# Four graph layers on one core: order and buffers at the seams, joined 64x64 sections, and attention weights divided before they are used

## The chip, the cores and the metric

The kernel runs on one core of one Trainium2 chip. Its time is the device time of one execution in microseconds (us); with one core this is the time of the slowest core. The engines are TensorE (PE; its weight loads are listed as PEld), VectorE (DVE), ScalarE (ACT), GpSimd (POOL) and SyncE (SP, which issues most DMAs). All data is fp32.

## The reference, cut to what matters

There are 128 graphs of 64 nodes with 512 features, 8192 tokens in all. Each of four layers takes `h = relu(layernorm(x))` and adds its result to x:

```python
# layer 0: one weight per node, softmax over the nodes of a graph
w = inv_scale * mask * sum_d(q * (adj @ (k * mask)));  x += softmax(w) * v
# layer 1: weight[i, j] = adj * exp(q_i . k_j), divided by its row sum
x += (weight / weight.sum(axis=2, keepdims=True)) @ value
# layer 2: eight heads of 64, scores times (adj + adj), softmax, output weights Wo
# layer 3: alpha = A * exp(leaky_relu(sj + si + ab)); transition = alpha / (sum + 1e-12)
H = X @ Wk[0] + (tr @ X) @ Wk[1] + (tr @ tr @ X) @ Wk[2] + bk;  x += relu(H)
```

## The kernel before, in words

The tokens form 32 blocks (`n_blk`) of 256: two tiles (`TT`) of 128 tokens, and each tile holds two graphs (`g`). Layers 0 and 1 alternate by pairs of blocks (list `steps`: layer 0 of blocks 0 and 1, layer 1 of blocks 0 and 1, layer 0 of blocks 2 and 3, and so on). Then layer 2 runs over all blocks, and layer 3 over all blocks. x goes to HBM between layers 1, 2 and 3.

Each 512x512 product is a `Product`: seven products of half size on combinations (`sums` of the block on POOL, `formed` or `chore` for the weights). `first`, `second` and `late` issue them, one `add` being four PE records of 128x256 or eight of 128x128; `keep_ab` and `keep_dc` read the PSUM banks in between, and `store`, `store_T` and `add_to` at the end. `side_by_side` runs two products together and calls the lists in `between`: the first list amid `first` and `second` of the first product, the others before each `late`.

Small matrices per graph are multiplied in the 64x64 form: `neighbour_sums` gives `pa` in layer 0, `po` in layer 1 (named po1 in the code) and `po` in layer 3 (po2 and po3 in the code). Layer 1's scores `sc` (`products`) have the form 128x64, layer 2's scores and contexts 64x64. `graph_sums` multiplies by a block diagonal of ones (form 128x128). Layer 1 makes `e` (the weights), sums its rows with four 64x1 products `den`, and scales the output by the reciprocal; layer 3 does so with `al`, in `layer3_tail` for po2, and the same reciprocal `r` serves `layer3_end` for po3.

PSUM has eight banks: pools `ps_tr` (2, transposes and small results), `ps_mm` (4, products) and `ps_sc` (2, scores and sums). Buffers in SBUF are named by tags and counts; a new tile waits for the oldest holder of its tag. The instruction order of each engine comes from a planner that follows the program's order as a priority and its own model of times; `tc.issue_after(ins)` puts what is traced inside it behind `ins` on that engine.

Names in the prediction's steps: `setup1` (L446) loads layer 1's q and k weights, makes nine dot products with the biases (L467), transposes both weights (`transpose_weight`, L416 to L422) and multiplies them (`folded`, L430). `add_to` (L333) is layer 2's residual addition. `setup3` (L733) multiplies `L3_WvT` by the two attention columns (`pu`). `layer3_norm` (L777) loads, normalises and makes the dots `hu` (L788), `di` and `sj`; `layer3_in` makes `sm_i` from di, then al, then in a second stage the transposes. `layer3_step` runs head, tail and the end of the block before.

## Time and profile before

| | |
|---|---|
| median of three runs | 2678.71 us (2675.41 to 2680.66) |
| the profiled execution | 2679.86 us, span 2678.1 us |
| mean granted clock of TensorE | 0.996 |
| PE busy, share of the span | 2639.5 us, 99% |
| DVE / ACT / POOL busy | 1702.8 / 947.7 / 1288.7 us |
| a pair of blocks in layers 0 and 1, from `den` to `den` | 60.22 us |
| a step of layer 3, from `den` to `den`, median | 21.98 us |

A row of the timeline has the start, the duration, the engine, the line, the operation, what it writes and reads, its form (`64*64` is the part of the array used), shapes and the number of merged records; an idle time and its releaser stand in brackets. Durations of matmuls overlap, so what a group costs is read from the distance to the next start. In the list of waits the three numbers are the total, the count and the longest.

### The profile page before, as it was taken

What the parts mean: (1) busy time and instruction counts of PE and PEld (TensorE: products, weight loads), DVE (VectorE), ACT (ScalarE), POOL (GpSimd) and SP (SyncE); (2) the same over time, 40 slices, a digit from 0 to 9 for tenths busy, and PEclk for the clock granted to TensorE, in tenths of its full rate; (3) what the DMA queues carried; (4) which work ended last, traced back from release to release, by engine and by line L of the source; (5) the groups of instructions that cost most, each with busy time, mean ns of one, the idle gap of its engine ahead of it and who ended that gap; (6) DMA issues with size and microseconds to landing.
All of it is one profiled execution on the core that took longest, in us unless ns stands there. A gap on an engine that the chain in (4) does not pass through costs nothing.

```text
span 2678.1 us, 52780 instructions
## 1 busy us (share of the span) xinstructions
PE 2639.5 (99%) x20752; PEld 2253.1 (84%) x20752; DVE 1702.8 (64%) x4398; ACT 947.7 (35%) x2290; POOL 1288.7 (48%) x1585
## 2 busy tenths in 40 slices
PE   8999999999999999999999999999899999999999
PEld 5888888888888889999999999999777777777776
DVE  5566666666666676566566566566566666666664
ACT  2333334333333333333333333333323333333332
POOL 3443333333433335656655655655464444445544
PEclk9999999999999999999999999999999999999999
DMA  5200111111111122111111111111111111111110
GB/s 158 67 35 34 35 35 35 42 43 35 50 34 35 34 66 78 45 45 39 45 45 39 45 45 39 45 45 45 65 50 51 51 51 51 51 51 51 51 50 32
DMA packets 103165, 129.80 MB, mean 48 GB/s; under 512 B 40835, under 2 KB 50051, under 8 KB 102917
## 3 DMA queue, kind: packets, MB, share of 16 engines
q1 hardware_dynamic: 102340, 125.38, 13.9%
q8 instruction: 163, 2.67, 0.4%
q10 hardware_dynamic: 576, 1.05, 0.1%
q14 instruction: 86, 0.70, 0.1%
HBM read 76.07 MB, written 50.34 MB: 47 GB/s over the span
## 4 chain that ended last, share of the span: by engine, by line
PE 81%; POOL 6%; DVE 5%; DMA 4%; ACT 3%; issue 2%; ACTq 0%; POOLq 0%; SPq 0%; DVEq 0%
PE ab_v L251 11%; PE ab_y L251 9%; PE dc_v L251 8%; PE dc_y L251 6%; PE ab_g L244 4%; PE ab_k L244 4%; PE ab_g L251 4%; PE ab_q L244 4%; PE tr L190 3%; PE dc_g L244 3%; PE dc_g L251 3%; PE po L392 3%; PE dc_k L244 3%; PE ab_o L251 3%; PE dc_q L244 3%; DMA x<-x 2%
## 5 line engine op out<-in xcount | busy, mean ns | idle before, releaser
L179 ACT ACTIVATE h<-x,nmr,rstd 128x512 f32<-128x512 f32 x256 | 194.4, 806 | 219.6 <-DVE nmr L174 211.0
L172 POOL TENSOR_TENSOR rstd<-ve,neghalf 128x2 f32<-128x2 f32 x128 | 89.8, 701 | 365.6 <-DVE ve L170 365.4
L167 DVE BATCH_NORM_STATS2 stats<-x 128x6 f32<-128x512 f32 x256 | 165.3, 677 | 74.6 <-DMA x<-x 68.4
L251 PE MATMUL ab_y<-L_Wk,hT 128*128 128x256 f32 x768 | 207.5, 393 | 4.1 <-DVE u_y L303 2.6
L251 PEld LDWEIGHTS ab_y<-L_Wk,hT 128*128 128x128 f32 x768 | 136.4, 190 | 77.4 <-issue 25.2
L251 PE MATMUL ab_v<-L_Wv,hT 128*128 128x256 f32 x768 | 200.7, 384 | 0.0
L251 PE MATMUL ab_y<-L_Wk,S 128*128 128x256 f32 x768 | 197.8, 380 | 0.0
L251 PE MATMUL dc_v<-L_Wv,S 128*128 128x256 f32 x768 | 197.3, 379 | 0.0
L251 PE MATMUL ab_v<-L_Wv,S 128*128 128x256 f32 x768 | 197.1, 379 | 0.0
L251 PE MATMUL dc_y<-L_Wk,S 128*128 128x256 f32 x768 | 192.9, 380 | 1.3 <-DVE u_y L859 1.2
L251 PEld LDWEIGHTS dc_y<-L_Wk,S 128*128 128x128 f32 x768 | 145.2, 190 | 23.2 <-DVE u_y L859 3.7
L251 PEld LDWEIGHTS ab_v<-L_Wv,S 128*128 128x128 f32 x768 | 145.9, 190 | 19.8
L880 POOL TENSOR_TENSOR tz<-tz,y 128x512 f32<-128x512 f32 x63 | 91.5, 1452 | 146.0 <-ACT tz L877 146.0
L251 PEld LDWEIGHTS ab_y<-L_Wk,S 128*128 128x128 f32 x768 | 144.1, 191 | 18.5
L251 PEld LDWEIGHTS dc_v<-L_Wv,S 128*128 128x128 f32 x768 | 143.4, 190 | 18.9 <-issue 0.8
L251 PEld LDWEIGHTS ab_v<-L_Wv,hT 128*128 128x128 f32 x768 | 135.9, 190 | 15.4
L190 PE MATMUL tr<-ident,h 128*128 128x128 f32 x1024 | 134.4, 275 | 0.0
L190 PEld LDWEIGHTS tr<-ident,h 128*128 128x128 f32 x1024 | 119.5, 142 | 10.5
L216 POOL TENSOR_TENSOR S<-hT 128x256 f32<-128x256 f32 x128 | 101.1, 790 | 35.0 <-ACT hT L193 34.7
L219 POOL TENSOR_TENSOR S<-hT 128x256 f32<-128x256 f32 x128 | 107.9, 843 | 1.2
L306 POOL TENSOR_TENSOR gv<-u_g,p_g 128x256 f32<-128x256 f32 x32 | 23.4, 730 | 174.4 <-DVE u_g L303 174.4
L217 POOL TENSOR_TENSOR S<-S,hT 128x256 f32<-128x256 f32 x128 | 101.0, 789 | 11.6 <-DVE ve L170 10.3
(238 smaller groups left out, 6433.8 us busy)
## 6 DMA issues: line engine op xcount, KB each, us to landing
x<-x SPq DMA_DIRECT2D x128, 512.0 KB, 3.5
x<-in_x_dram SPq DMA_DIRECT2D x32, 512.0 KB, 3.6
out_dram<-x SPq DMA_DIRECT2D x31, 512.0 KB, 2.8
adjT<-in_adjT_dram SPq DMA_DIRECT2D x64, 64.0 KB, 1.9
adjq<-in_adj_dram SPq DMA_DIRECT2D x64, 64.0 KB, 2.3
L_Wk<-in_L_Wk_dram SPq DMA_DIRECT2D x16, 256.0 KB, 4.7
L_Wv<-in_L_Wv_dram SPq DMA_DIRECT2D x12, 256.0 KB, 5.3
q<-in_L_Wqk_dram ACTq DMA_DIRECT2D x4, 256.0 KB, 6.1
```

The costliest lines, as they stand in the source:

```text
L167: nc.vector.bn_stats(stats[:, t, :], x[:, t, :])
L172: nc.gpsimd.tensor_tensor(rstd, ve, neghalf, ALU.pow)
L179: nc.scalar.activation(h, x[:, t, :], AF.Relu, bias=nmr[:, t : t + 1], scale=rstd[:, t : t + 1])
L190: nc.tensor.transpose(pt[:, k, :], h[:, k * P : (k + 1) * P], ident)
L216: nc.gpsimd.tensor_tensor(S1, A21, A22, ALU.add)
L217: nc.gpsimd.tensor_tensor(S2, S1, A11, ALU.subtract)
L219: behind[0] = nc.gpsimd.tensor_tensor(S3, A11, A21, ALU.subtract)
L244: nc.tensor.matmul(dst[:, m * P : (m + 1) * P], w[:, place, k, m * P : (m + 1) * P], left[:, k, :], start=key not in self.begun, stop=last ...
L251: nc.tensor.matmul(dst, left[:, k, :], w[:, place, k, :], start=key not in self.begun, stop=last and k == 1, skip_group_check=True,)
L306: nc.gpsimd.tensor_tensor(y[:, 1, F:], self.u3, self.p5, ALU.add)
L392: nc.tensor.matmul(ps[t][half[g ^ t]], e[half[g], t, :], us[t][half[g]], start=True, stop=True)
L880: nc.gpsimd.tensor_tensor(tz[t], tz[t], y0[:, t, :], ALU.add)
```

## The change

The transposes of layer 1's q and k weights get different PSUM banks, and ACT copies all of q's; the nine dot products are made during block 0's products, and layer 0's end of block 0 is issued amid the folding. In layers 1 and 3 the weights `e` and `al` are divided by their sums ahead of use: `graph_sums`, a reciprocal of 128x128 and a product replace `den` and the scaling at the output. Layer 1's neighbour sums are issued ahead of the next odd block's `sc` or `pa` (`before`), layer 3's po3 ahead of the next block's po2. Layer 2's additions on DVE come ahead of POOL's second addition to the same part. `L3_WvT` is loaded into other buffers, `sm_i` and the division get later places, and layer 3's dots are split from its norm and issued behind the block's last read of PSUM. The first block's `am` and `msc` are issued behind the first norm's steps.

```diff
+    behind_norm = {}
     def norm(x, name: str):
...
-        nc.gpsimd.tensor_tensor(rstd, ve, neghalf, ALU.pow)
+        by_rows = nc.gpsimd.tensor_tensor(rstd, ve, neghalf, ALU.pow)
...
-        nc.vector.scalar_tensor_tensor(nmr, mv[:, :, 0], -1.0, rstd, ALU.mult, ALU.mult)
+        scaled = nc.vector.scalar_tensor_tensor(
+            nmr, mv[:, :, 0], -1.0, rstd, ALU.mult, ALU.mult
+        )
+        behind_norm.setdefault(0, (by_rows, scaled))
...
-            nc.gpsimd.tensor_tensor(x[:, 1, :F], self.u3, x[:, 1, :F], ALU.add)
-            nc.vector.tensor_tensor(x[:, 0, F:], self.c, x[:, 0, F:], ALU.add)
...
+            self.taken = nc.vector.tensor_tensor(x[:, 0, F:], self.c, x[:, 0, F:], ALU.add)
+            nc.gpsimd.tensor_tensor(x[:, 1, F:], self.u3, x[:, 1, F:], ALU.add)
...
-                x[:, 1, F:], self.u3, x[:, 1, F:], ALU.add
+                x[:, 1, :F], self.u3, x[:, 1, :F], ALU.add
...
     def side_by_side(*parts, between=()):
...
-    def transpose_weight(w, name: str):
-        pts = [ps_mm.tile([P, K, P], FP, tag="mm", name=f"tw_{name}_{m}") for m in range(K)]
+    def transpose_weight(w, name: str, places=((ps_mm, "mm"),) * K, on_scalar=(1, 3)):
+        pts = [
+            pool.tile([P, K, P], FP, tag=tag, name=f"tw_{name}_{m}")
+            for m, (pool, tag) in enumerate(places)
+        ]
...
-            if m % 2:
+            if m in on_scalar:
...
-    def folded(aT, bT, layer: int, place: int):
+    elsewhere = ((ps_tr, "tr"), (ps_sc, "sc")) * 2
+    def folded(aT, bT, layer: int, place: int, amid=lambda: None):
...
+            if not i:
+                amid()
...
     def setup0():
...
-        nc.vector.tensor_scalar(msc, mcol, -(float(D) ** -0.5), None, ALU.mult)
+        with tc.issue_after(behind_norm[0][1].ins):
+            nc.vector.tensor_scalar(msc, mcol, -(float(D) ** -0.5), None, ALU.mult)
...
     def setup1():
...
+        dots((d, bias[:, 0], 1))
+        dots(*((u[:, k : k + 1], x, 1) for k, x in enumerate(columns(qT))))
+        yield
+        dots(*((cc[:, k : k + 1], x, 0) for k, x in enumerate(columns(kT))))
...
-        for w, c in zip((qT, kT), "qk"):
-            transpose_weight(w, f"{c}1")
-        m = folded(kT, qT, 1, 2)
+        yield
+        transpose_weight(qT, "q1", on_scalar=range(K))
+        transpose_weight(kT, "k1", elsewhere)
+        m = folded(kT, qT, 1, 2, lambda: layer0_end(0, *softmax))
...
         yield m, u, c1, d, w1v, w2
-    def layer0(b: int, x, adjT, hs, hT, between):
+    def layer0(b: int, x, adjT, hs, hT, between, before):
...
-        am = small.tile([P, TT, N], FP, tag="am", name=f"am_{b}", bufs=2)
-        nc.gpsimd.tensor_tensor(
-            am,
-            adjT,
-            mcol[:, b * TT : (b + 1) * TT].unsqueeze(2).to_broadcast([P, TT, N]),
-            ALU.mult,
-        )
-        pa = [ps_tr.tile([P, D], FP, tag="tr", name=f"pa_{b}_{t}") for t in range(TT)]
+        am = small.tile([P, TT, N], FP, tag="am", name=f"am_{b}", bufs=3)
+        with tc.issue_after(behind_norm[0][0].ins):
+            nc.gpsimd.tensor_tensor(
+                am,
+                adjT,
+                mcol[:, b * TT : (b + 1) * TT].unsqueeze(2).to_broadcast([P, TT, N]),
+                ALU.mult,
+            )
+        before()
+        pa = [
+            pool.tile([P, D], FP, tag=tag, name=f"pa_{b}_{t}")
+            for t, (pool, tag) in enumerate((
+                ((ps_sc, "sc"), (ps_sc if b % 2 else ps_mm, "sc" if b % 2 else "mm"))
+                if b else ((ps_tr, "tr"),) * 2
+            ))
+        ]
...
-    def layer1(b: int, x, adjT, hs, hT, between):
+    def layer1(b: int, x, adjT, hs, hT, between, before):
...
+        before()
...
+    def layer1_divided(b: int, e):
+        den = graph_sums(e.rearrange("p t i -> p (t i)"), TT * N, f"1_{b}")
+        r = small.tile([P, TT, N], FP, tag="r", name=f"r1_{b}", bufs=2)
+        nc.vector.reciprocal(r.rearrange("p t i -> p (t i)"), den)
+        nc.vector.tensor_tensor(e, e, r, ALU.mult)
     def layer1_end(b: int, x, v, e, to):
-        po = [ps_sc.tile([P, D], FP, tag="sc", name=f"po1_{b}_{t}") for t in range(TT)]
-        den = [ps_tr.tile([P, 1], FP, tag="tr", name=f"den1_{b}_{t}") for t in range(TT)]
-        for t in range(TT):
-            for g in range(2):
-                nc.tensor.matmul(
-                    den[t][half[g ^ t]], e[half[g], t, :], ones_bd[half[g], g * N : g * N + 1],
-                    start=True, stop=True,
-                )
-        parts = neighbour_sums(po, e, [v[:, t, :] for t in range(TT)])
-        r = small.tile([P, TT], FP, tag="r1", name=f"r1_{b}")
-        for t in range(TT):
-            nc.vector.reciprocal(r[:, t : t + 1], den[t])
-        for t, out_at, at in parts:
-            nc.vector.scalar_tensor_tensor(
-                x[out_at, t, :], po[t][at], r[at, t : t + 1], x[out_at, t, :], ALU.mult, ALU.add
-            )
+        po = [ps_tr.tile([P, D], FP, tag="tr", name=f"po1_{b}_{t}") for t in range(TT)]
+        for t, out_at, at in neighbour_sums(po, e, [v[:, t, :] for t in range(TT)]):
+            nc.vector.tensor_tensor(x[out_at, t, :], po[t][at], x[out_at, t, :], ALU.add)
...
-        cT = big.tile([P, K, T], FP, tag="hT", name=f"cT_{b}")
+        cT = big.tile([P, K, T], FP, tag="hT" if b + 1 < n_blk else "v", name=f"cT_{b}")
...
-        halves = []
-        for i in range(2):
-            w = big.tile([P, K // 2, D], FP, tag="v", name=f"w3vT_{i}")
-            nc.sync.dma_start(
-                w,
-                a["L3_WvT"][i * D // 2 : (i + 1) * D // 2, :].rearrange("(k p) o -> p k o", p=P),
-            )
-            halves.append(w)
+        pair = big.tile([P, 2, D], FP, tag="v", name="w3vT")
+        chunks = [pair[:, k, :] for k in range(2)] + [
+            med.tile([P, D], FP, tag="agg", name=f"w3vT_{k}", bufs=2) for k in range(2, K)
+        ]
+        for k, w in enumerate(chunks):
+            nc.sync.dma_start(w, a["L3_WvT"][k * P : (k + 1) * P, :])
...
-            for to, x in ((pu, halves[k // 2][:, k % 2, :]), (pc, bv[:, k : k + 1])):
+            for to, x in ((pu, chunks[k]), (pc, bv[:, k : k + 1])):
...
-        us2 = big.tile([2, D + 1], FP, tag="v", name="us2")
-        nc.scalar.copy(us2[:, :D], pu)
-        nc.scalar.copy(us2[:, D:], pc)
+        us2 = med.tile([2, D], FP, tag="h", name="us2", bufs=6)
+        cs2 = small.tile([2, 1], FP, tag="cc", name="cs2", bufs=1)
+        nc.scalar.copy(us2, pu)
+        nc.scalar.copy(cs2, pc)
...
-        nc.sync.dma_start(urow, us2)
+        nc.sync.dma_start(urow[:, :D], us2)
+        nc.sync.dma_start(urow[:, D:], cs2)
...
     def layer3_norm(b: int, source):
...
+        return x, adjT, norm(x, f"3_{b}")
+    def layer3_dots(b: int, x, adjT, hs):
...
-        hs = norm(x, f"3_{b}")
...
-        al = small.tile([P, TT, N], FP, tag="am", name=f"al_{b}", bufs=2)
+        al = small.tile([P, TT, N], FP, tag="am", name=f"al_{b}", bufs=3)
...
         yield
         made.append((x, al, sums(transposed(hs, f"3_{b}"), f"3_{b}")))
+        yield
+        den = graph_sums(al.rearrange("p t i -> p (t i)"), TT * N, f"al_{b}")
+        r = small.tile([P, TT * N], FP, tag="r", name=f"r3_{b}", bufs=2)
+        nc.vector.tensor_scalar(r, den, 1e-12, None, ALU.add)
+        nc.vector.reciprocal(r, r)
+        nc.vector.tensor_tensor(al, al, r.rearrange("p (t i) -> p t i", t=TT), ALU.mult)
         yield
     def layer3_head(b: int, ops, between):
...
         p.first(ops, w3[0])
+        yield
         p.second(ops, w3[0])
-        den = [ps_tr.tile([P, 1], FP, tag="tr", name=f"den3_{b}_{t}") for t in range(TT)]
-        for t in range(TT):
-            for g in range(2):
-                nc.tensor.matmul(
-                    den[t][half[g ^ t]], al[half[g], t, :], ones_bd[half[g], g * N : g * N + 1],
-                    start=True, stop=True,
-                )
+        yield
         po = [ps_sc.tile([P, D], FP, tag="sc", name=f"po2_{b}_{t}") for t in range(TT)]
         parts = neighbour_sums(po, al, [y[:, 1, t, :] for t in range(TT)])
-        r = small.tile([P, TT], FP, tag="r1", name=f"r3_{b}")
-        for t in range(TT):
-            nc.vector.tensor_scalar(r[:, t : t + 1], den[t], 1e-12, None, ALU.add)
-        nc.vector.reciprocal(r, r)
         for t, to, at in parts:
-            nc.vector.scalar_tensor_tensor(
-                y[to, 0, t, :], po[t][at], r[at, t : t + 1], y[to, 0, t, :], ALU.mult, ALU.add
-            )
+            nc.vector.tensor_tensor(y[to, 0, t, :], po[t][at], y[to, 0, t, :], ALU.add)
...
-        nc.vector.tensor_tensor(y0[:, 0, F:], p.c, p.u2, ALU.add)
+        kept = nc.vector.tensor_tensor(y0[:, 0, F:], p.c, p.u2, ALU.add)
...
-        yield r, y0
-    def layer3_end(b: int, x, al, y, r, y0):
-        po = [ps_sc.tile([P, D], FP, tag="sc", name=f"po3_{b}_{t}") for t in range(TT)]
+        yield y0, kept
+    def layer3_end(b: int, x, al, y, y0):
+        po = [ps_tr.tile([P, D], FP, tag="tr", name=f"po3_{b}_{t}") for t in range(TT)]
...
         for t, out_at, at in neighbour_sums(po, al, [y[:, 0, t, :] for t in range(TT)]):
             if last and not t:
-                nc.vector.scalar_tensor_tensor(
-                    tz[t], po[t], r[:, t : t + 1], y0[:, t, :], ALU.mult, ALU.add
-                )
+                nc.vector.tensor_tensor(tz[t], po[t], y0[:, t, :], ALU.add)
...
-                nc.scalar.activation(tz[t][out_at], po[t][at], AF.Copy, scale=r[at, t : t + 1])
+                nc.scalar.copy(tz[t][out_at], po[t][at])
...
-    transpose_weight(f0[1], "k0")
+    transpose_weight(f0[1], "k0", ((ps_sc, "sc"),) * 2 + ((ps_mm, "mm"),) * 2)
...
-    open_end = []
...
     for i, (layer, b) in enumerate(steps):
...
+        between = [[], [chore], []]
+        if i == 0:
+            for n in (1, 2):
+                between[n].append(lambda: next(setup))
...
+            begun = []
             made1 = next(setup)
-        between = [[], [chore], []]
-        for n, end in open_end:
+        for n, end in begun:
...
+        begun = []
         if i + 1 < len(steps):
...
         if layer == 0:
-            softmax = layer0(b, *loaded[b], *normed[i], between)
-            open_end = [(0, lambda b=b, softmax=softmax: layer0_end(b, *softmax))]
+            softmax = layer0(b, *loaded[b], *normed[i], between, open_end if b % 2 else nothing)
+            begun = [(0, lambda b=b, softmax=softmax: layer0_end(b, *softmax))]
         else:
-            attention = layer1(b, *loaded[b], *normed[i], between)
-            open_end = [
-                (1, lambda b=b, a=attention: layer1_end(b, loaded[b][0], *a, x1[b]))
-            ]
-            if b == n_blk - 2:
-                open_end.append((1, lambda: fetch2(2)))
+            v, e = layer1(b, *loaded[b], *normed[i], between, open_end if b % 2 else nothing)
+            begun = [(1, lambda b=b, e=e: layer1_divided(b, e))]
+            def open_end(b=b, v=v, e=e):
+                layer1_end(b, loaded[b][0], v, e, x1[b])
+                if b == n_blk - 2:
+                    fetch2(2)
...
     def layer3_step(b: int, ahead: bool = True):
+        nonlocal normed3
...
         stages = layer3_in(b + 1, *normed3, made_in) if b + 1 < n_blk else iter(())
...
-            next(stages, None)
             if b + 2 < n_blk and ahead:
                 normed3 = layer3_norm(b + 2, x2[b + 2])
-        y = layer3_head(b, ops, [[begin], [ending.pop()], [lambda: next(stages, None)]])
+        y = layer3_head(b, ops, [
+            [begin], [], [lambda: next(stages, None), lambda: next(stages, None)]
+        ])
         yield
         tail = layer3_tail(b, al, ops, y)
         next(tail)
         yield
-        r_y0 = next(tail)
-        ending.append(lambda: layer3_end(b, x, al, y, *r_y0))
+        next(stages, None)
+        next(tail)
+        yield
+        ending.pop()()
+        next(tail)
+        yield
+        y0, kept = next(tail)
+        ending.append(lambda: layer3_end(b, x, al, y, y0))
+        if b + 2 < n_blk and ahead:
+            with tc.issue_after(kept.ins):
+                normed3 = layer3_dots(b + 2, *normed3)
         yield
...
-        [lambda: prepare2(1), chore], [*(end for _, end in open_end), chore], [lambda: turned2(1)]
+        [lambda: prepare2(1), chore], [begun[0][1], chore], [open_end, lambda: turned2(1)]
...
             stages = layer3_in(0, *normed3, made_in)
-            next(stages)
         if b + 1 < n_blk:
-            qk, ops = layer2_in(b + 1, normed2[b + 1], [[], [lambda: chore(1 if b else 2)]])
+            qk, ops = layer2_in(b + 1, normed2[b + 1], [
+                [], [lambda: chore(1 if b else 2), lambda: next(stages, None)]
+            ])
...
         else:
-            next(parts)
+            for _ in range(3):
+                next(parts)
         (of_o,) = side_by_side(part)
...
+        next(stages, None)
         nc.sync.dma_start(tokens(x2[b]), x)
...
-        if b >= n_blk - 3:
-            normed3 = layer3_norm(b - n_blk + 3, x2[b - n_blk + 3])
+        if n_blk - 3 <= b < n_blk - 1:
+            normed3 = layer3_dots(
+                b - n_blk + 3, *layer3_norm(b - n_blk + 3, x2[b - n_blk + 3])
+            )
+        elif b == n_blk - 1:
+            with tc.issue_after(of_o.taken.ins):
+                normed3 = layer3_dots(2, *layer3_norm(2, x2[2]))
```

`dots` issues the same `scalar_tensor_tensor` with `accum_out` as before, and `nothing` does nothing.

## The prediction

> **What bounds the kernel now.** I read the page first, then the waits of PE, then PE's timeline through the places that they name, and last the windows for the granted clock.
>
> ```profile
> PE 2639.5 (99%) x20752; PEld 2253.1 (84%) x20752; DVE 1702.8 (64%) x4398; ACT 947.7 (35%) x2290; POOL 1288.7 (48%) x1585
> ```
>
> TensorE sets the time; nothing else passes two thirds. A gain has to come off PE's own row: idle time, work at half clock, or time that one of its instructions takes only because of its neighbours. Waits of PE:
>
> ```profile
> PE sm_i L400 <- DVE di L793: 3.4, 1, 3.4
> PE tw_k L416 <- DVE q L422: 3.3, 1, 3.3
> PE ab_y L251 <- DVE u_y L303: 2.6, 1, 2.6
> PE pu L754 <- DMA w3vT<-in_L_WvT_dram: 2.6, 1, 2.6
> PE tr L690 <- ACT hT L193: 1.7, 1, 1.7
> PE ab_k L244 <- DVE x L341: 1.7, 8, 0.2
> PE dc_y L251 <- POOL L_Wk L99: 1.2, 1, 1.2
> ```
>
> (The last three numbers of a row are total, count and longest.) All but one are single waits, at the seams between layers. The windows around the largest (columns: length, then busy time and instructions of PE, PEld, DVE, ACT and POOL, granted clock, DMA share, GB/s):
>
> ```profile
> 43.10:57.70 14.60, 7.34 (x43) 4.85 (x41) 13.00 (x31) 3.83 (x9) 1.81 (x3) 0.75 0.02 1
> 1883.00:1890.00 7.00, 4.42 (x13) 1.79 (x13) 0.00 (x0) 1.03 (x4) 2.52 (x3) 0.77 0.46 155
> 1917.00:1925.00 8.00, 4.59 (x27) 4.42 (x26) 5.21 (x12) 0.69 (x3) 6.13 (x6) 0.79 0.18 66
> 1996.00:2003.50 7.50, 4.87 (x16) 3.71 (x16) 5.98 (x17) 1.78 (x5) 4.57 (x6) 0.77 0.41 143
> ```
>
> Each such stall also costs clock. Now an ordinary stretch of layers 0 and 1, and one of layer 3; the first number is the start, and I measure by the distance of starts:
>
> ```profile
> 424.56 1.03 PE L251 MATMUL dc_v<-L_Wv,hT 128*128 128x256 f32 x4
> 425.52 0.29 PE L581 MATMUL den<-ones_bd,e 64*64 64x1 f32 x8
> 425.66 1.07 PE L392 MATMUL po<-v,e 64*64 64x512 f32 x8
> 426.66 1.13 PE L251 MATMUL ab_g<-fold,hT 128*128 128x256 f32 x4
> 427.62 1.03 PE L251 MATMUL ab_g<-fold,S 128*128 128x256 f32 x4
> ...
> 435.76 0.38 PE L400 MATMUL sm_w<-wd,ones_bd 128*128 128x128 f32 x2
> 435.98 1.03 PE L251 MATMUL ab_g<-fold,S 128*128 128x256 f32 x4
> ...
> 2210.61 1.03 PE L251 MATMUL dc_y<-L_Wk,S 128*128 128x256 f32 x4
> 2211.63 1.13 PE L251 MATMUL ab_y<-L_Wk,hT 128*128 128x256 f32 x4
> 2212.60 1.03 PE L251 MATMUL ab_y<-L_Wk,S 128*128 128x256 f32 x4
> ```
>
> A group of four 128x256 products takes 0.865 us between its like. Ahead of a 64x64 section it takes 0.96, and so does the first group behind it (426.66 to 427.62): 0.095 + 0.10 for going in and out. The section itself takes 1.00, of which two streams of 512 columns (0.43 each, as the folding products show) are 0.86. So of a section on its own about 0.30 us is edge. `den` takes 0.14, about 0.02 of it edge that the section would have anyway; a 128x128 sum 0.22. The last three rows are layer 3's small stall: 1.02 instead of 0.865, and 0.97 after it.
>
> **The change, part by part** (minus is faster).
>
> 1. *Setup of layer 1.* From 43.12 to 72.97 us PE does 32 transposes (2 x 1.75), one `pa` section (1.2), one sum (0.22) and 32 folding records (32 x 0.43 = 13.8): 18.7 us of work in 29.85. The excess, 11.2, is the nine dot products of 1.04 us that hold DVE from 46.4 to 54.9 while copies of q and k wait behind them, and the half clock after. Now they are made during block 0's products, where DVE works 4.9 of 13 us (30 to 43); q and k of layer 1 are issued at 29.2 to 32.9 and land some 4 us later, so there is room for most of the 9.4. k's transposes get other banks, ACT takes all q copies (4 x 0.55 = 2.2, ending near 47.3), then two k copies (to 48.4): a wait of about 1.8 stays, giving -9.4. If the dots push DVE's copies further back, -5; if the wait is filled, -11. I take -8.5.
> 2. *Layers 0 and 1.* Sections per pair of blocks fall from five to three: po+sc+pa, po+pa, sc. po beside pa, both 64x64, saves 0.30; po beside sc (128x64) shares only the 128-side edges, 0.20 (as sc to pa already does). 15.5 pairs x 0.50 = -7.7. `den` goes: 32 x 0.12 = -3.8. A 128x128 sum comes: 32 x 0.22 = +7.2. Together -4.3. DVE adds per block a 128x128 reciprocal. The rows give 0.16 us for 1 column, 0.20 for 8, so 6 ns a column: 0.92 as an estimate, at least 0.28 (another 128x128 operation), at most twice the estimate; I take 0.92. With a 0.29 product and two small reciprocals less, +0.9. It hides under the half step of other products before po; without that it would cost 32 x 1.2 = 38 us. Stores of x1 and the load of block 2 move later by up to one step behind others on SP; each issue is 0.4 us on a queue nearly empty, and four x buffers hold. Nothing.
> 3. *Layer 2.* In the residual addition DVE waited for POOL (80.7 us over 31 blocks) with four PSUM reads behind it. The reorder lets DVE read a, d and c first and puts the two POOL additions of u3 behind. PE gets what it lost on this: the wait row shows eight waits, and the distances of starts at those places are 0.3 long each, with 0.1 in the group after: -3.0 (at most -3.5; zero if another wait ends there last). POOL issues the same operations, only the last ones a little later; x2's store behind them waits for the same sum as before.
> 4. *L3_WvT.* Its second half waited for a v buffer. From 1882.49 to 1890.56 PE needs 3.5 us of work and takes 8.07. Four DMAs in place of two, none waiting, plus one for the extra row (5 x 0.4 on SP, idle there): -4.5. The two L3_bk rows now wait for those buffers; they are first needed some 90 us later.
> 5. *Seam to layer 3.* `sm_i` of block 0 moves behind eight groups of 0.89, to about 1922.7 on the old scale, while di was ready at 1920.8: excess 5.2 (8.14 for 2.90 of work) goes. The u_o wait at 1911 (1.7) has its dots in place still: half, -0.9. Norm 2 is queued behind the last block's addition, so hT copies (1.9), POOL's chores (1.4) and S_c (1.1, now with three more stretches before it) are free; pc loses po as neighbour, +0.3: -3.7 taken. The stall at 1996.7 (2.8, and 1.6 at half clock) was four dots ahead of u_y; they move to the end of the step: -3.4. Sum -13.2.
> 6. *Layer 3, steady.* po3 and po2 become one section: 31 x 0.30 = -9.3; `den` -3.8; sums +7.2: -5.9. The small stalls, taken over all steps from the distances of starts, are 8.5 us (median step 21.98, 21.76 without them). Dots move behind `kept`, norm's rows start later: -5. The output store and, through the x buffer that it frees, the load of x two blocks ahead go later on SP: ACT copies, tz on POOL, relu and store end some 6 us into the next step, so x lands near 10 and h near 13 of 21.6. Its dots come at the end of that step, its sum and transposes 9.5 us into the next; were that slack of 10 us missing, the transposes would stall PE in every step. End: POOL has block 30's two tz additions (2.6) among the last block's: +0.7.
> 7. *New waits* that no row shows: division in DVE's and POOL's way (0.15 in half of layer 3's steps, as today's small stall: 2.5), sections waiting for their banks (2), dots of block 2 just before its sum (1): +5.5, between 0 and 20.
>
> Order of am, rstd and msc at the start: nothing, since h's transposes come behind q's, which wait for DMA until 8.3; 0.3 if that cover were gone. Sum: -8.5 -4.3 -3.0 -4.5 -13.2 -5.9 -5 +0.7 +5.5 = -38.2. The profiled execution took 2679.86 (span 2678.1 and 1.8 around it): 2641.7. The median shown is 1.2 lower; I say 2641.
>
> **Two rules of the Trainium skill.** The window 1883 to 1890 shows half clock after a stall of 2.6 us, as does 1996. The page "TensorE: Matmul & The Clock Gate" (Why this matters for your kernels) asks only that there be no idle gaps above about 3 us. By the page two of my seams would give back the stall alone, 3.3 us less in sum; I follow the rows, while stalls of 1.2 to 1.9 kept full clock here.
> Against the change speaks "TensorEngine Tiling (Array Packing)" (PSUM Bottleneck): packed products are not evacuated any faster, so copies can become the limit. Two joined sections leave three ACT copies (0.59) and three DVE additions (0.75) at once. By the rule y0's banks come late. By the rows: from the section's start to y1's first product are 2.1 + 2.7 + 3.5 = 8.3 us; DVE needs until about 7.0 (additions to 4.3, two relu steps 1.4, four reads 1.4). No stall, 1.2 us to spare; were it missing, each microsecond would be 31.
>
> **Rivals.** *Half the seams* (0.22): a repaired wait uncovers the next, as the DVE and ACT queues are written out of order by the planner; parts 1, 3, 4, 5 bring 13 instead of 29, the joins and stalls 9: 2657. For: DVE was busy in three of the four windows. Against: the causes differ, so do the remedies.
> *Slower* (0.09): layer 3's sum over al comes about 5.4 us after `sm_i`. Today that chain (sm_i 2208.66, al done 2215.9) takes 7.2. If it stays so, PE waits 1.8 in 31 steps, +56, in all 2697. It decides from 1.3 us a step (6.7). Against: 3.4 of it is di behind dots and y0 reads, 1.3 al's buffer held by po3; both are changed, leaving 3 to 4.
> *Not what it says* (0.05): the planner leaves a 128 product between the sections; 17 us are lost, half the seams too: 2657 + 17 = 2674.
>
> **Numbers.** About 0.2% (5.4 us) is what a measurement can tell from no change. Likeliest (0.64): 2641. Faster 0.64 + 0.22 = 0.86, same 0.05, slower 0.09. Part 7's ends, part 1's ends and the half-seam case give 2628 to 2666.
>
> **What would show it.** Right: a pair of blocks falls from 60.22 to 59.95, a layer-3 step from 21.98 to about 21.6; no `den`; po rows of 16 records or two adjacent; clock 1.00 in the four windows; fold's end near 64 us. Wrong: PE waits on al or `sm_al`, on u_y in every step, or tw_k still behind DVE.

## The result and the profile after

The changed kernel takes 2675.48 us (median of 22 runs, 2673.3 to 2678.21) against 2679.05 (22 runs of the kernel before). The ratio is 0.9988, 95% interval 0.9981 to 0.9994: faster by 3.6 us, where 38 were forecast. The profiled execution has a span of 2673.9 us.

The waits of PE in the changed kernel (total, count, longest) show first that the seams went and something else came:

```profile
PE ab_y L256 <- DVE u_y L286: 22.4, 29, 0.8
...
PE ab_o L256 <- DVE u_o L286: 1.5, 1, 1.5
PE po L397 <- DVE y L863: 1.1, 2, 0.8
PE sm_w L405 <- ACT k L421: 0.6, 1, 0.6
PE sm_al L405 <- DVE al L833: 0.5, 2, 0.2
```

The long single waits `sm_i` 3.4, `tw_k` 3.3, `pu` 2.6 and the 2.6 for u_y are gone. In their place stands u_y in 29 steps, the sign that the prediction had named as its refutation. The stretches that answer to the four windows of before (length, busy time and instructions of PE, PEld, DVE, ACT, POOL, granted clock, DMA share, GB/s) confirm it: PE is full and the clock is 1.00 in all four.

```profile
43.80:62.70 18.90, 18.21 (x67) 9.67 (x65) 8.84 (x25) 6.34 (x16) 4.43 (x6) 1.00 0.07 15
1861.00:1870.00 9.00, 9.00 (x61) 5.84 (x60) 1.89 (x5) 1.62 (x5) 7.02 (x8) 1.00 0.36 109
1895.00:1905.00 10.00, 10.00 (x87) 9.88 (x86) 6.68 (x16) 2.31 (x7) 8.46 (x8) 1.00 0.15 55
1954.00:1980.00 26.00, 26.00 (x134) 21.36 (x132) 19.68 (x49) 8.58 (x18) 11.02 (x14) 1.00 0.18 61
```

Where the gain was lost shows when starts of the same PE instruction are compared in the two timelines:

| from the span's start to | before | after | this stretch alone |
|---|---|---|---|
| layer 1's first product (first `dc_g<-S,fold`) | 85.93 | 76.81 | -9.1 |
| layer 2's first product (`dc_q`) | 1020.02 | 1008.12 | -2.8 |
| the group behind the second po2 of layer 3 | 2005.98 | 1973.75 | -20.3 |
| the end | 2678.1 | 2673.9 | +28.0 |

Up to the second block of layer 3 the kernel is 32.2 us ahead; the 30 steps behind it give 28.0 back. A step of layer 3 is 22.92 (before: 21.98; forecast: about 21.6). That the sign of the forecast came out right rests on the small remainder of the two. One such step on PE (start, duration):

```profile
2293.21 1.95 PE L397 MATMUL po<-y,al 64*64 64x512 f32 x16
...
2300.37 1.03 PE L256 MATMUL dc_y<-L_Wk,hT 128*128 128x256 f32 x4
2301.48 1.13 PE L256 MATMUL dc_y<-L_Wk,S 128*128 128x256 f32 x4
...
2304.17 1.03 PE L256 MATMUL dc_y<-L_Wk,hT 128*128 128x256 f32 x4
2305.97 1.13 PE L256 MATMUL ab_y<-L_Wk,hT 128*128 128x256 f32 x4 [0.78 <-DVE u_y L286]
```

The joined section is there: 16 records in 1.88 us (2293.21 to 2295.09). But from 2300.37 to 2301.48 is 1.11 and from 2304.17 to 2305.97 is 1.80, where such groups cost 0.865, and the group behind each costs 0.1 more: 1.38 us a step; the 29 steps behind the seam take 22.91 to 23.56. DVE in the same step, from the section on:

```profile
2296.29 1.74 DVE L891 SCALAR_TENSOR_TENSOR x<-tz,x 128x512 f32<-128x512 f32 x1 [2.64 <-POOL tz L890]
2297.96 0.68 DVE L863 TENSOR_TENSOR y<-po,y 128x512 f32<-128x512 f32 x1
2298.56 0.68 DVE L891 SCALAR_TENSOR_TENSOR x<-tz,x 128x512 f32<-128x512 f32 x1
2299.26 1.39 DVE L863 TENSOR_TENSOR y<-po,y 64x512 f32<-64x512 f32 x2
2300.67 0.43 DVE L870 TENSOR_TENSOR y<-ab_y,bs 128x256 f32<-128x256 f32 x1
2301.01 0.41 DVE L871 TENSOR_TENSOR u_y<-ab_y,p_y 128x256 f32<-128x256 f32 x1
...
2301.87 0.42 DVE L874 TENSOR_TENSOR y<-dc_y,u_y 128x256 f32<-128x256 f32 x1
2302.20 0.68 DVE L805 SCALAR_TENSOR_TENSOR hu<-h,u 128x512 f32<-128x512 f32 x1
...
2305.51 0.41 DVE L286 TENSOR_TENSOR u_y<-ab_y,p_y 128x256 f32<-128x256 f32 x1
```

Read it downwards: the relu step of the block before (`x<-tz`) stands first in DVE's queue and waits for POOL's addition, while po2's sums are ready behind it. It takes 1.74 us. Then come po2's reading, the other relu step, and only then the four reads of y0's banks. The second of them (L871) ends at 2301.42, just ahead of the late `dc_y` at 2301.48, and `kept` (L874) is the last, at 2302.29, 9.1 us after the section's start. The four dots (L805) follow `kept`, and u_y comes behind them, 0.9 after PE could have used it.

### The profile page after: what moved, and what is told of

It is laid out like the page before. It is cut to its first block, busy times and chain, and to the rows that moved or that the text cites. A ratio compares the mean times of both kernels' runs of the same rounds, so it can differ in the third digit from the quotient of the medians.

```text
span 2673.9 us, 51906 instructions
## 1 busy us (share of the span) xinstructions
PE 2629.0 (98%) x20368; PEld 2261.9 (85%) x20368; DVE 1778.0 (66%) x4396; ACT 934.5 (35%) x2292; POOL 1280.7 (48%) x1585
## 4 chain that ended last, share of the span: by engine, by line
PE 82%; DVE 12%; POOL 2%; DMA 2%; ACT 1%; issue 1%; SPq 0%; POOLq 0%; ACTq 0%; DVEq 0%
PE ab_v L256 12%; PE dc_v L256 9%; PE ab_y L256 7%; PE dc_y L256 4%; PE ab_g L249 4%; PE ab_k L249 4%; PE tr L195 4%; PE ab_q L249 4%; PE ab_o L256 4%; PE ab_g L256 4%; PE dc_g L249 3%; PE dc_g L256 3%; PE dc_k L249 3%; PE dc_q L249 3%; PE dc_o L256 3%; DVE hu L805 3%
## 5 line engine op out<-in xcount | busy, mean ns | idle before, releaser
L891 DVE SCALAR_TENSOR_TENSOR x<-tz,x 128x512 f32<-128x512 f32 x64 | 76.2, 1191 | 83.3 <-POOL tz L890 83.2
L285 ACT COPY p_y<-ab_y 128x256 f32<-128x256 f32 x96 | 35.8, 373 | 250.3 <-PE ab_y L256 250.1
```

What stands on the lines that cost most here:

```text
L285: nc.scalar.copy(self.p1, self.a)
L891: nc.vector.scalar_tensor_tensor(x[:, t, :], tz[t], 0.0, x[:, t, :], ALU.max, ALU.add)
```

## The experiments

Steps of layer 3 are given as the median distance between `sm_i` sums. "Traced" means placed in the program's order, from which the planner then makes each engine's own. Three pieces of VectorE's work are moved about: the relu steps `x<-tz` with the store (R), the norm of the block two ahead (N), and its dots (D). The kernels of part 1, and the one without relu in part 2, start from the changed one.

**1. What in the step is late.**

D free of `kept`:

```diff
-            with tc.issue_after(kept.ins):
-                normed3 = layer3_dots(b + 2, *normed3)
+            normed3 = layer3_dots(b + 2, *normed3)
```

> Base: the changed kernel (2675.5 us). One edit: layer 3's four dots are no longer issued behind the block's last read of y0 (`kept`), so that u_y can follow these reads at once on VectorE; the order of the relu steps (x<-tz ahead of po2's and y0's readings) is kept. The changed kernel's step of layer 3 is 22.92 us; TensorE loses about 1.0 of it at ab_y (waits for u_y behind the dots) and 0.35 at dc_y (waits for y0's bank). Theory 1, both the dots' place and the relu's place cost, each its own stall: the ab_y part goes, step about 21.9, 30 steps x 1.0 = -30, time about 2645. Theory 2, everything comes from the relu steps that wait for GpSimd ahead of po2's reading: the dots only fill time, u_y stays late, 2670 to 2676. Theory 3, the dots matter alone: both stalls go, step 21.55, about 2634.

Measured: 2696.85 us, step 23.57, 21 slower. All three theories missed. Waits of PE:

```profile
PE ab_y L256 <- DVE u_y L308: 18.5, 28, 0.7
PE dc_y L256 <- DVE u_y L871: 10.8, 29, 0.9
```

The planner put the dots earlier, as soon as h was made, and there they stand ahead of y2's reads (u_y L308); the wait for y0 (u_y L871) stayed. The pin behind `kept` is no cause but a protection.

R behind `kept`, as a second stage of `layer3_end`:

```diff
                 nc.gpsimd.tensor_tensor(tz[t], tz[t], y0[:, t, :], ALU.add)
+        yield
+        for t in range(TT):
             nc.vector.scalar_tensor_tensor(
...
-        ending.pop()()
+        end = ending.pop()()
+        next(end)
...
+        with tc.issue_after(kept.ins):
+            next(end, None)
```

> Base: the changed kernel (2675.5 us). One edit: the two relu steps x<-tz of the block before (they wait for GpSimd's addition) and its store are issued behind `kept`, no longer ahead of po2's reading; the dots stay behind `kept` too. Theory 1 (each order costs its own stall): y0's reads come 3 to 4 us earlier, so the dc_y stall goes, and u_y, though behind dots and relu, comes 2 us before it is needed; step about 21.55 to 21.6, time about 2634. Theory 2 (the relu's place is the whole cause): the same 2634. Theory 3 (the dots are the whole cause): the ab_y stall stays, since now relu and dots both stand ahead of u_y; 2665 to 2676.

Measured: 2656.45 us, ratio to before 0.9914 (0.9898 to 0.9931), step 22.32. Both old stalls are gone, so the relu's place was their cause, but about half of what they cost goes to a new one:

```profile
PE sm_al L405 <- DVE al L833: 19.1, 28, 2.3
```

Between `sm_i` and al DVE now has norm's steps, since the next x lands late: DVE waits 68.1 us for it in 29 steps, where it waited 2.2 in the changed kernel.

Both edits:

> Base: the changed kernel. Both edits together: dots free, relu steps behind `kept`. Theories 1 and 2: step about 21.55, time about 2634, no better than the relu edit alone since its stalls are gone already. If the dots are still a burden when the relu is late: some 5 to 15 us below the relu edit alone. If the dots, placed by the planner, fall ahead of al's chain, `sm_al` waits in each step: above 2650.

Measured: 2758.18 us, step 25.86, and 80.9 us of waits of `sm_al` for al: the case that the last sentence allowed for. The dots ran amid al's chain.

The other direction, po3 in a section of its own again, as before the change:

```diff
-            [begin], [], [lambda: next(stages, None), lambda: next(stages, None)]
+            [begin], [ending.pop()], [lambda: next(stages, None), lambda: next(stages, None)]
...
-        ending.pop()()
```

> Base: the changed kernel. One edit: layer 3's po3 goes back to where it was before the change, a 64x64 section of its own between y2's and y1's products of the next block; the joined section, and with it the relu steps ahead of po2's reading, are undone, all else (divided al, dots behind `kept`) stays. If the joined section is what brings VectorE's lateness: +0.30 of edges a step, about -1.3 of stalls, 30 x -1.0 = -30, about 2645. If the dots' place is the cause: edges only, 2675 + 9 = 2684.

Measured: 2642.11 us, ratio to before 0.9862 (0.9847 to 0.9876), step 21.88. PE waits for u_y in one step of layer 3 only. One join, meant to save 0.30 us of edges a step, had cost 33 us in all. The dots are still behind `kept` here and stall nothing, so their place costs only where `kept` is late already.

**2. What the joined section needs.** Relu and the addition to x left out in all blocks but the last, as a bound:

```diff
-                nc.gpsimd.tensor_tensor(tz[t], tz[t], y0[:, t, :], ALU.add)
...
+                nc.gpsimd.tensor_tensor(x[:, t, :], tz[t], y0[:, t, :], ALU.add)
```

> Base: the changed kernel (2675.5). In all blocks but the last the relu step of layer 3 is left out: GpSimd's addition writes the stored block itself, so this output lacks relu and x. The joined section, the dots behind `kept` and all other orders stay. If the two relu steps ahead of po2's reading are the whole loss of a step: step 21.57 to 21.6 in place of 22.92, 30 x 1.3, about 2635. If the dots' place has a part of its own: ab_y still waits for u_y, about 2650 to 2665. If the joined section's own readings are too slow whatever stands ahead: 2675.

Measured: 2655.21 us, step 22.37: the middle case by the number, but not for its reason. `kept` ends 5.7 us after the section's start, yet u_y is late again, for it waits 1.84 us for ACT's p_y:

```profile
2301.53 0.42 DVE L286 TENSOR_TENSOR u_y<-ab_y,p_y 128x256 f32<-128x256 f32 x1 [1.84 <-ACT p_y L285]
```

ACT made h (1.52 us) ahead of p_y, for norm had run some 2 us earlier in the step. So the relu was not all; norm's place has a price of its own. The next kernel keeps R behind `kept` and traces N behind al's chain, loads unchanged:

```diff
-            [begin], [], [lambda: next(stages, None), lambda: next(stages, None)]
+            [begin], [], [lambda: next(stages, None), lambda: next(stages, None), normal]
```

> Base: the kernel with the relu steps behind `kept` (2656 us), whose step of layer 3 still loses about 0.6 us because al comes late for `sm_al`: its load of x, and with it the norm's steps (two of them held up beside GpSimd, one waiting for it), stand in VectorE's queue between `sm_i` and al. One edit more: the norm of the block two ahead is traced behind al's chain, its loads stay where they were. If those norm steps are what makes al late: no wait at `sm_al`, step 21.57 to 21.6, 30 x 0.7 less, about 2635. If al is late for another reason (relu and dots ahead of `di`): 2650 to 2656. If the norm, now later, makes the dots late for the next `sm_i`: above 2660.

Measured: 2646.54 us, step 22.10, in the first two behind the seam 21.52. No wait at `sm_al`: norm was what held al. About 0.55 a step was left. I took it for u_y behind relu and dots and tried both.

R traced in the next step's head:

```diff
         def begin():
+            for end in relus:
+                next(end, None)
...
-        with tc.issue_after(kept.ins):
-            next(end, None)
+        relus.append(end)
```

> Base: the kernel with relu behind `kept` and norm behind al's chain (2646.5 us; step about 22.08, its first steps 21.52). What is left there is read as u_y: behind `kept` VectorE makes two relu steps (1.8) and four dots (2.6) before u_y, which comes 0.3 late. Edit: the relu steps and the store of the block before are traced in the next step's head. If the relu ahead of u_y is what is left: step 21.52 to 21.6, about 2632. If x, stored 3 to 5 us later, now lands too late for norm and dots: `sm_i` or ab_y waits, 2650 or more.

Measured: 2675.67 us, step 22.92. Nothing is learned: DVE's order shows the relu ahead of po2's reading again (1.74 us, after 2.62 of waiting), for without the pin the planner put it there. It repeats the changed kernel.

D traced in the next head, behind y2's u_y and still behind `kept`:

```diff
-            [begin], [], [lambda: next(stages, None), lambda: next(stages, None), normal]
+            [begin], [dotted], [lambda: next(stages, None), lambda: next(stages, None), normal]
...
+                with tc.issue_after(last_kept[0].ins):
+                    normed3 = layer3_dots(b + 1, *normed3)
```

> The same base (2646.5). Edit: the four dots are traced in the next step's head, behind u_y of y2, still not ahead of `kept`; the relu steps stay behind `kept`. u_y then comes about 2.6 us earlier, di about 0.4 us later, 2 us ahead of its sum. If the order of dots and u_y is what is left: step 21.52 to 21.6, about 2632. If di becomes late: `sm_i` waits and the step stays above 22, 2646 or more.

Measured: 2646.38 us, step 22.08: no change, and ab_y no longer waits. So it was not u_y. In this kernel the section takes 2.41 in place of 1.88, and DVE shows why:

```profile
2300.79 0.16 DVE L176 SCALAR_TENSOR_TENSOR nmr<-mv,rstd 128x2 f32<-128x2 f32 x1 [1.97 <-POOL rstd L174]
2300.86 0.42 DVE L308 TENSOR_TENSOR u_y<-ab_y,p_y 128x256 f32<-128x256 f32 x1
```

Norm's last step waits for POOL's rstd with y1's reads queued behind it, and po2 needs y1. Two ways to take that away: norm pinned behind y1's reads, or x earlier through a fifth buffer.

```diff
+            self.read = nc.vector.tensor_tensor(y[:, 0, F:], self.c, self.u2, ALU.add)
...
+        with tc.issue_after(of_y1.read.ins):
+            normal()
```

> Base: the kernel with relu behind `kept`, norm behind al's chain and dots in the next head (2646.4). In its steady steps the joined section takes 2.41 in place of 1.88, since VectorE stands 1.97 us at nmr, waiting for GpSimd's rstd, ahead of y1's last reads, which po2 needs. Edit: norm is issued behind y1's reads. If that wait is what is left of the joined section's price: step 21.52 to 21.6, about 2632. If nmr now holds up po2's reading and y0's banks: ab_y or dc_y waits, step 22 or more, 2646 or above.

Measured: 2630.71 us, ratio to before 0.9817 (0.9802 to 0.9832), the fastest of all. Every step behind the seam is 21.52 or 21.53. The same stretch of DVE now has po2's reading ahead of the relu:

```profile
2295.61 0.68 DVE L176 SCALAR_TENSOR_TENSOR nmr<-mv,rstd 128x2 f32<-128x2 f32 x1 [0.57 <-POOL rstd L174]
2296.22 0.28 DVE L843 TENSOR_TENSOR al<-al,r 128x128 f32<-128x128 f32 x1
2296.93 2.09 DVE L865 TENSOR_TENSOR y<-po,y 128x512 f32<-128x512 f32 x3 [0.43 <-PE po L397]
...
2300.24 0.42 DVE L876 TENSOR_TENSOR y<-dc_y,u_y 128x256 f32<-128x256 f32 x1
2300.57 2.01 DVE L895 SCALAR_TENSOR_TENSOR x<-tz,x 128x512 f32<-128x512 f32 x2
```

With the section at 2294.94, `kept` (L876 here) ends 5.7 us after it. The joined section itself is sound: with it in place, edits of order alone brought the step from 22.92 to 21.52.

Five x buffers, on the kernel with D in the next head, and on the one with R alone:

```diff
-        x = big.tile([P, TT, D], FP, tag="x", name=f"x{stage}_{b}", bufs=4)
+        x = big.tile([P, TT, D], FP, tag="x", name=f"x{stage}_{b}", bufs=5)
```

> The same base (2646.4), whose x lands only 12 us after the section before, since its load waits for the store of the block whose buffer it takes, and that store now waits for the late relu. Edit: five x buffers in place of four, so that the load waits for the store of one block earlier. If x's late landing drives norm into al's and y1's way: norm runs earlier, nmr's wait for rstd goes or moves to a free place, step 21.52 to 21.7, 2632 to 2637. If the place in the program's order decides, not the data: unchanged, 2646.

> Base: the kernel with the relu steps behind `kept` alone (2656.5; `sm_al` waits for al 19.1 us in 28 steps, because x lands late and norm's steps stand ahead of al). Edit: five x buffers in place of four, nothing else. If the late load is the cause of that wait: no wait at `sm_al`; what is left is u_y behind relu and dots, step 21.6 to 22, 2635 to 2646. If norm's place in the program's order is the cause: unchanged, about 2656.

Measured: 2646.75 and 2647.63 us, steps 22.09 and 22.08. On the first it changes nothing, and x still lands late (DVE waits for it up to 3.8 us), so the buffer's holder was not its gate. SP's queue shows another: the load stands behind the store of the block before, which waits for the relu (375.6 us in 31 steps), and is issued 2.8 us after it with four buffers and with five. On the second al comes in time, though x lands no earlier; what is left is the wait of nmr for rstd again, 55.3 us in 30 steps, as on the first. In its trace nmr stands behind al in DVE's queue, where it stood ahead with four buffers: another order of the planner, not an earlier load. Why the buffer's count changes that order is open.

**3. The parts that gained.** Each undone in the changed kernel.

Layer 1's neighbour sums in a section of their own, first in the transposes' banks, then (the lower edit too) in those of `sc`:

```diff
+            begun.append((2, open_end))
...
-        po = [ps_tr.tile([P, D], FP, tag="tr", name=f"po1_{b}_{t}") for t in range(TT)]
+        po = [ps_sc.tile([P, D], FP, tag="sc", name=f"po1_{b}_{t}") for t in range(TT)]
```

> Base: the changed kernel (2675.5). One edit: layer 1's neighbour sums get a section of their own amid the next block's second product (no longer joined with `sc` or `pa`); division by the sums ahead of use stays. By the prediction's step 2 the joins are worth 0.50 us a pair of blocks: pair 59.88 to 60.38, time +7.7, about 2683. If the gain of a pair came from elsewhere (the missing `den`, order of queues): 2675 to 2678. If joined sections save the full edges on both sides, 0.30 each: pair +0.60, 2685.

> Base: the changed kernel (2675.5). Layer 1's neighbour sums have a section of their own again, as in the run that came out at 2700, but in the banks of `sc`, so that the transposes behind them need not wait for VectorE's readings (7.2 us of waits there, and their group split). If the prediction's edges hold (0.50 us a pair): pair +0.50, about 2683. If the section's place itself costs more: nearer 2700. If edges are worth nothing: 2676.

Measured: 2700.19 us and 2682.03. In the first the edit brought a stall of its own, so it says nothing of edges (its layers 0 and 1 take 25.0 us longer, of which this row explains 7.2):

```profile
PE tr L195 <- DVE x L607: 7.2, 32, 0.4
```

The second is clean: layers 0 and 1 take 937.74 us from layer 1's first product to layer 2's instead of 931.31, +6.4. In the regular pairs of blocks it is 0.47 a pair (60.35 instead of 59.88), where 0.50 was forecast.

The nine dot products, traced behind block 0 again, then with their old buffers too (both edits):

```diff
-        if i == 0:
-            for n in (1, 2):
-                between[n].append(lambda: next(setup))
...
-                junk = med.tile([P, P, K], FP, tag="e2", name="bias1", bufs=3)
+                junk = med.tile([P, P, K], FP, tag="agg", name="bias1", bufs=2)
```

> Base: the changed kernel (2675.5). One edit: layer 1's nine dot products are traced behind block 0 again, ahead of the transposes of q and k; the new PSUM banks and ACT's copies of q stay. If the dots' place is what the setup gained from: layer 1's first product comes 7 to 9 us later (76.8 to about 85), time about 2683. If the banks and ACT's copies were the gain: 1 to 3 us later, 2677.

> Base: the changed kernel (2675.5). The nine dot products are traced behind block 0 (which alone changed nothing: they ran from 31.7 to 40.9 us all the same) and their results go to the old home again, the two buffers of `agg` that block 0 holds until 46. If the buffers' home decides when they run: they run after 46 us as before the change, and layer 1's first product comes 5 to 9 us later, about 2682. If the new PSUM banks and ACT's copies suffice: within 2 us, 2675 to 2677.

Measured: 2675.22 us with layer 1's first product at 76.18, and 2686.85 with it at 86.06. The place in the program was worth nothing; the planner had them run from 31.7 us on all the same. The buffers decide: the change had also moved the dots' products from tag `agg` to tag `e2`, and in the `agg` buffers they wait for block 0's sums (free at about 46 us). The dots read q and k, and the copies of the transposes overwrite q and k in place, so the copies wait for the dots, ACT's as well as DVE's:

```profile
53.09 0.80 PE L405 MATMUL sm_w<-wd,ones_bd 128*128 128x128 f32 x2 [6.89 <-ACT k L421]
```

```profile
52.45 0.59 ACT L421 COPY k<-tw_k 128x512 f32<-128x512 f32 x1 [1.41 <-DVE bias L471]
```

```profile
54.13 1.27 DVE L423 COPY k<-tw_k 128x512 f32<-128x512 f32 x2
```

PE waits for the bank that ACT's copy of k frees, ACT for a dot, and DVE's own copies come behind the last one. With the old buffers the new PSUM banks and ACT's copies are worth nothing (86.06, and 85.93 before); what the new buffers give without the new banks was not run.

## Why the prediction was wrong, and where it was right

- **Step 1**, -8.5: -9.1. The mechanism was right, its lever was not named: the dots' new buffers. Their place in the program alone is worth nothing, and the banks and copies alone nothing either.
- **Step 2**, -4.3: -2.8 up to layer 2's first product. A pair of blocks is 59.88 (59.95 forecast) over 14 pairs, -4.8; the last pair gives 2.0 back, which no run explains. The join is worth 0.47 a pair (0.50 in the sum). The reciprocal of 128x128 that I estimated at 0.92 takes 0.94 (L840 in the groups of DVE).
- **Steps 3 to 5**, -20.7 together: -20.3. Layer 2's first eight blocks fell from 29.10 to 28.63, 3.8 where 3.0 was forecast, and all four windows run at full clock. The u_o wait, of which half was to go, stayed as it was: 1.47 us before and after.
- **Step 6, the one that failed**: "Dots move behind `kept`, norm's rows start later: -5", with -5.9 for the joined section. Measured +28.0 together with step 7, against -4.7. The section's own part was right: stall-free, the step is 21.52, and 21.88 without the join, so it is worth 0.36 (0.30 in the sum, though the terms that the prediction reads from the rows, 0.095, 0.10 and 0.14, make 0.335).
- **The term that was mis-sized** stands in the place on packed products: "DVE needs until about 7.0", counted as additions to 4.3, two relu steps of 1.4 and four reads of 1.4. It needs 9.1. The relu was placed behind the additions and at 0.69 each; it stands ahead of them, waits for POOL until 3.1 us after the section's start (the sums could be read at 2.0), and takes 1.74 the first time. That is 1.1 and 1.0, and with them the 1.2 to spare were gone. Moving the relu behind `kept`, and nothing else, took both old stalls away. The sentence beside it, that each microsecond missing would be 31, was the right price: 1.38 lost a step times 30 is 41. u_y behind the dots, which makes 1.0 of the 1.38, was not in the sum at all. The warning of the Trainium skill (TensorEngine Tiling (Array Packing), PSUM Bottleneck), that packed products are not evacuated any faster, pointed to the right place: `dc_y` comes 0.25 us late for y0's bank in each step. But the rate of the reads was not the limit, since with another order the same section frees the banks in 5.7 us; I set the warning against a count that held no wait.
- **Step 7**, +5.5 between 0 and 20: the stalls of steady layer 3 are 41. The list had banks and division, but no queue in which an early instruction waits for another engine.
- **The rival "slower"** did not occur: `sm_al` waits 0.5 us in all, as the division had room. It did in the kernels with a late relu (19.1 and 80.9 us), through norm and dots ahead of al. "Half the seams" did not occur: no seam uncovered another. Nor did "not what it says": the rows of 16 records are there.
- **A reading and a sum that do not hold.** Not all stalls of 1.2 to 1.9 us kept full clock. In the setup before, PE stood 1.45 and 1.22 us, and in a third stall, of 1.19, the granted clock fell (the columns are those of the windows above):

```profile
47.60:50.30 2.70, 1.15 (x6) 0.72 (x6) 2.70 (x6) 0.59 (x1) 0.00 (x0) 1.00 0.01 3
50.40:52.20 1.80, 0.97 (x4) 0.71 (x4) 1.80 (x5) 0.59 (x1) 0.00 (x0) 0.50 0.00 0
```

The stall of 3.3 came only then, while a single one of 1.47 (1912 to 1917) left the clock at 1.00. So in these traces the length of the longest single gap does not tell when the clock falls. And 32 sums of 0.22 are 7.0, not 7.2; it changes nothing.

## What to carry to other kernels

When a section is joined to another, everything that hangs on it moves along: here an ACT copy, a POOL addition and a DVE relu came into the one stretch in which DVE has to free the banks of the next product. Before such a move, write down the order of the reading engine's queue in that stretch, with what each entry waits for, not only the sum of its durations. An edit to the order is made only where the trace shows the new order: two of these kernels had another order in the program and ran like the one they came from.

## What the runs showed of the hardware

The relu step `x<-tz` (128x512) took 0.69 us in the kernel before; in the changed one the first of each step takes 1.74 and the second 0.68. These are the groups of DVE after, then before (count, then busy time and mean ns):

```profile
L891 DVE SCALAR_TENSOR_TENSOR x<-tz,x 128x512 f32<-128x512 f32 x64 | 76.2, 1191 | 83.3 <-POOL tz L890 83.2
```

```profile
L881 DVE SCALAR_TENSOR_TENSOR x<-tz,x 128x512 f32<-128x512 f32 x64 | 44.3, 693 | 88.9 <-POOL tz L880 88.8
```

POOL's two additions of tz in that step:

```profile
2294.99 2.49 POOL L890 TENSOR_TENSOR tz<-tz,y 128x512 f32<-128x512 f32 x2 [0.45 <-ACT tz L887]
```

The second runs from about 2296.24 to 2297.48. The relu that starts at 2296.29 ends at 2298.03, 0.55 after it. The other relu, with POOL idle, takes 0.68. The other steps and kernels show the same. In 31 steps of the changed kernel the first relu starts inside POOL's addition, takes 1.74 and ends 0.55 us after it; in the fastest kernel relu steps that start later inside one of POOL's additions take 1.21 or 0.88, and nearly all end 0.54 to 0.55 us after it too. In the kernel before the relu starts first, and then it is POOL that loses: its addition takes 1.65 to 1.67 in 30 steps, in place of 1.27.

```profile
2217.61 0.69 DVE L881 SCALAR_TENSOR_TENSOR x<-tz,x 128x512 f32<-128x512 f32 x1 [1.72 <-POOL tz L880]
```

```profile
2217.77 1.66 POOL L880 TENSOR_TENSOR tz<-tz,y 128x512 f32<-128x512 f32 x1 [0.20 <-ACT tz L877]
```

This is the rule of the Trainium skill, page "SBUF — State Buffer" (Who interferes with whom): a DVE instruction with two inputs in SBUF contends with a GpSimd instruction that reads SBUF, and the second to start is blocked until the first is through. The traces agree in both directions, though a blocked relu ends sooner after the addition than its full 0.68. The prediction had no such term, and by this rule, as an estimate, the first relu beside the second addition of tz costs up to one POOL addition of 1.2 us more, near the 1.0 that was missing. The block alone is not the loss: with po3 in a section of its own the first relu takes 1.78 us in 30 steps, and PE waits for nothing behind it.
